# Graph attention with experts: scores of two heads by one weight load, and list tests as signs on ScalarE

## The chip, the core and the metric

The kernel runs on one core of a Trainium2 chip. The core has engines with queues of their own, which meet through semaphores: PE multiplies matrices into PSUM, with weight loads counted apart as PEld; DVE and POOL work on vectors; ACT applies functions element by element; SP (SyncE) mainly starts transfers (DMA). A transfer by a list of row numbers (a gather) is started by POOL. The metric is the device time of the whole program in microseconds (us). The kernel before takes 2405.32 us, the median of three runs from 2403.5 to 2418.53.

## What is computed

A layer of graph attention over 4096 nodes with 512 features, then a mixture of experts, both with a residual. Cut to what matters:

```python
# x: (4096, 512), adj: (4096, 4096) of zeros and ones
def attention(n, adj, Wks, Wqs, Wvs, Wo):            # 8 heads of 64
    adj = maximum(adj, eye)
    q, k, v = (einsum('nd,hdk->hnk', n, W) for W in (Wqs, Wks, Wvs))
    scores = einsum('hqk,hmk->hqm', q, k) * 64 ** -0.5
    scores = scores + 0.01 * eye - 1e16 * (1 - adj)
    return einsum('hqm,hmk,hko->qo', softmax(scores), v, Wo)

x = x + attention(layernorm(x), adj, ...)
x = x + experts(layernorm(x), ...)                   # top 2 of 8, GELU
```

The adjacency matrix is sparse, and its density falls from the first nodes to the last. The kernel works on 32 tiles of 128 queries and visits only the keys that a query of the tile has as neighbours.

## The kernel before

**Stage one** makes keys, values and queries, and beside that a list of keys for each tile of queries. It runs in 64 slots: four slots of each eight project keys and values of 128 tokens, four project queries and normalize the next tokens. An adjacency tile of 2 MB is loaded every 13/8 slots. DVE reduces it, two slots later, to flags: has this key a neighbour in the first 64 queries, in the last 64? Keys are then listed in three sections: those of the first half alone, those of both, those of the second half alone.

A list is made for four tiles at a time (a group). From running counts of the flags along the 32 keys that a partition holds (`x_g`) and the count before each partition (`base`), a list slot's row is found by a product: `started` has a one where partition p has begun at list slot s, and `dx` holds the step of each quantity from one partition to the next.

```python
def count_3(g):
    b = ...                                     # keys before partition p, by section
    nc.vector.scalar_tensor_tensor(lo, hi, -float(P), b, op0=ALU.mult, op1=ALU.add)   # L419
    ...
    base[g] = b

def steps(g):
    nc.tensor.matmul(pd, step, x_g, start=True, stop=False, ...)
    nc.tensor.matmul(pd[:, 1:], corner, x_g[:, :2], start=False, stop=True, ...)
    nc.tensor.matmul(pe, step, x_g[:, 2], start=True, stop=True)
    dx = lp.tile([P, 4, G, NX], BF16, tag="dx", ...)
    nc.scalar.copy(dx[:, :3], pd)
    nc.scalar.copy(dx[:, 3], pe)

def begun(i):                                   # L457
    for k, (t0, t1) in enumerate(ranges(i)):    # up to three ranges of list slots
        nc.gpsimd.tensor_scalar(
            started[i, k], slots[:, t0 * P : t1 * P], base[g][:, k, j : j + 1], None,
            op0=ALU.is_ge,
        )

def list_rows(i, k):                            # L476, on PE
    of = [(0, 0)] if h == 0 else [(2, 3)] if h == 1 else [(0, 0), (1, 1), (2, 2)]
    for n, (q, r) in enumerate(of):
        nc.tensor.matmul(pr[:, t, :], started[i, q][:, s], row_x[g][:, r, j, :], ...)

def list_keys(i, k):                            # from L486, on DVE
    ...
    nc.vector.tensor_copy(key_of[:, to], key)   # L502
    nc.vector.tensor_scalar_add(mask_of[:, u], k, float(i * (N + 1)))      # L510
    # or, for a half: nc.vector.tensor_scalar(mask_of[:, u], k, 2.0, ...)  # L512
```

A group's list takes eight slots. In each, the first part comes ahead of the slot's projections, and what the function returns comes behind them:

```python
def lists_at(g, s):
    if s == 0:
        count_1(g)
        return [lambda: count_2(g)]
    if s == 1:
        count_3(g); begun(i)
        return [lambda: steps(g)]
    if s == 2:
        begun(i + 1)
        return []
    if s == 3:
        return [lambda: rows(i)]
    if s == 4:
        keys(i); begun(i + 2)
        return [lambda: rows(i + 1)]
    ...
```

Once a list is ready, POOL gathers some of its mask rows in advance (`pack`, up to three a slot), and SP writes them to DRAM in one piece, to be loaded later without a gather. `load_adj`, L345, starts from SP at the head of a slot; `neighbours`, L352, is the reduction.

**Attention** goes through the listed keys of each tile in steps of 128, after a step for the tile's own keys. A step in a one-sided section (a half step) has 64 queries, the others have 128. `AHEAD` steps before, the keys and values (`kv`) and the mask are fetched. PE then turns the keys (`pk`, L893), multiplies them with the queries (`s`, L922), and after the exponential on ACT (L932) and the mask on DVE (L941) multiplies the result with the values (`po`, L954):

```python
def load_q(i):
    q_in[i] = qp.tile([P, NP, P], F32, tag="q", ...)      # NP = 4 pairs of heads
    nc.sync.dma_start(out=q_in[i], in_=qT_d[:, :, ts(i, P)])

def scores(n):
    s = [ps_s.tile([P, NP, P], F32, tag="s", ...) for r in range(2)]
    for p in range(NP):
        for r in range(2):                                # head 2p + r
            rows = slice(r * KD, (r + 1) * KD)            # its 64 rows
            nc.tensor.matmul(                             # L922
                part(s[r], i, c)[:, p, :], k[rows, p, :], q_in[i][rows, p, q],
                start=True, stop=True,
            )
    ...
    for r in range(2):
        nc.scalar.activation(e[:, r * NP : (r + 1) * NP], part(s[r], i, c), AF.Exp)  # L932

def values(n):
    for p in range(NP):
        for r in range(2):
            h = 2 * p + r
            nc.tensor.matmul(                             # L954
                po[i][r * KD : (r + 1) * KD, p, q], v[:, ts(h, KD)], e[:, r * NP + p, :], ...
            )
    nc.vector.tensor_add(acc[i][:, :, q], acc[i][:, :, q], e)
```

Each product of 32-bit numbers stands in the profile as two loads of weights and two multiplications. At a tile's end, `sums` (L979), `rb` (L992: four products of 128 rows by 128 columns with 128 columns streamed) and `py` (L1001) finish it. Routing of the tokens and the **experts** follow (from L1295), which the change leaves alone.

Of the kernel before, what the change touches and what calls it, by code (L numbers as in the profile page):

```python
# [10 lines left out]
F32 = mybir.dt.float32  # L11
# [9 lines left out]
P = 128  # L21
# [22 lines left out]
def kernel(  # L44
# [174 lines left out]
    def load_q(i):  # L219
        q_in[i] = qp.tile([P, NP, P], F32, tag="q", name=f"q_{i}")  # L220
        nc.sync.dma_start(out=q_in[i], in_=qT_d[:, :, ts(i, P)])
# [46 lines left out]
    with tc.tile_pool(name="wqkv", bufs=1) as wp, tc.tile_pool(name="p1", bufs=3) as work, tc.tile_pool(  # L268
# [39 lines left out]
        )  # L308

# [21 lines left out]
        def list_constants():  # L331
            nc.vector.tensor_sub(step, ident, step)
            nc.vector.tensor_mul(other, other, part)
            nc.vector.tensor_scalar(other, other, -1.0, 1.0, op0=ALU.mult, op1=ALU.add)
            nc.vector.memset(again_c, 1.0)
            nc.vector.memset(again_c[:, :, :, 0:1], 0.0)
            nc.vector.tensor_scalar_mul(corner, corner, -1.0)
            for k in range(KV // D):
                nc.sync.dma_start(out=kv_d[N : N + 1, ts(k, D)], in_=blank[:1, :D])
# [60 lines left out]
        def count_3(g):  # L400
# [24 lines left out]
            base[g] = b  # L425

        def steps(g):

# [3 lines left out]
            nc.tensor.matmul(  # L432
                pd[:, 1:], corner, x_g[:, :2], start=False, stop=True, skip_group_check=True
            )
            pe = ps_l.tile([P, G, NX], F32, tag="l", name=f"pe_{g}")
            nc.tensor.matmul(pe, step, x_g[:, 2], start=True, stop=True)
            dx = lp.tile([P, 4, G, NX], BF16, tag="dx", name=f"dx_{g}")
            nc.scalar.copy(dx[:, :3], pd)
            nc.scalar.copy(dx[:, 3], pe)
# [7 lines left out]
        def begun(i):  # L447

            g, j = divmod(i, G)
            for k, (t0, t1) in enumerate(ranges(i)):  # L450
                if t0 == t1:
# [5 lines left out]
                nc.gpsimd.tensor_scalar(  # L457
                    started[i, k], slots[:, t0 * P : t1 * P], base[g][:, k, j : j + 1], None,
                    op0=ALU.is_ge,
# [5 lines left out]
        def list_rows(i, k):  # L465
# [4 lines left out]
            for t in range(m):  # L470
                h = half_of(i, t0 + t)

                of = [(0, 0)] if h == 0 else [(2, 3)] if h == 1 else [(0, 0), (1, 1), (2, 2)]
# [8 lines left out]
        def list_keys(i, k):  # L482
# [21 lines left out]
            for h, u0, u1 in ((0, 0, a), (None, a, b), (1, b, listed[i])):  # L504
                u0, u1 = max(u0, t0), min(u1, t0 + m)
                if u0 < u1:
                    u = slice(at[i] + u0, at[i] + u1)
                    k = key[:, u0 - t0 : u1 - t0]
                    if h is None:
                        nc.vector.tensor_scalar_add(mask_of[:, u], k, float(i * (N + 1)))  # L510
                    else:
                        nc.vector.tensor_scalar(  # L512
# [27 lines left out]
        def lists_at(g, s):  # L540

            def rows(i):
                for k in range(len(chunks(i))):
                    list_rows(i, k)
                    if k:
                        list_keys(i, k - 1)
# [3 lines left out]
            if s == 0:  # L550
                count_1(g)
                return [lambda: count_2(g)]
            if s == 1:
                count_3(g)
                begun(i)
                return [lambda: steps(g)]
            if s == 2:
                begun(i + 1)
                return []
            if s == 3:  # L560
                return [lambda: rows(i)]
            if s == 4:
                keys(i)
                begun(i + 2)
                return [lambda: rows(i + 1)]
            if s == 5:
                keys(i + 1)
                begun(i + 3)
                return [lambda: rows(i + 2)]
            if s == 6:  # L570
                keys(i + 2)
                return [lambda: rows(i + 3)]
            keys(i + 3)
            return []
# [40 lines left out]
        def pack():  # L615
            i, c = ready.pop(0)
            m = work.tile([P, P], F32, tag="mask", bufs=6, name=f"pm_{i}_{c}")
# [5 lines left out]
        lists_from = {13 * (g * G + G - 1) // 8 + 3: g for g in range(NTB)}  # L623
        for u in range(8 * NTB + 1):
# [4 lines left out]
            for k in range(8):  # L629
                if u - k in lists_from:  # L630
                    due += lists_at(lists_from[u - k], k)
# [19 lines left out]
            if u - 2 in load_at:  # L651
                neighbours(load_at[u - 2])
                if load_at[u - 2] == NT - 1:
# [4 lines left out]
                    q_cm = tc.tile_pool(name="q", bufs=2, side="right")  # L658
                    qp = q_cm.__enter__()
                    load_q(0)  # L660
# [6 lines left out]
            if u - 8 in lists_from:  # L667
                g = lists_from[u - 8]
                ready += [
                    (i, c) for i in range(g * G, g * G + G) for c in range(listed[i])  # L670
                    if c % 5 in (1, 3)
                ]
# [29 lines left out]
    def route_1(m, l, pool, name):  # L702
# [4 lines left out]
        ahead = pool.tile([P, m, E, E], F32, tag="ahead", name=f"ahead_{name}")  # L707
        nc.vector.tensor_tensor(ahead, other, own, op=ALU.is_gt)
        same = pool.tile([P, m, E, E], F32, tag="same", name=f"same_{name}")
# [133 lines left out]
    with tc.tile_pool(name="p2a", bufs=2) as two, tc.tile_pool(  # L843
# [38 lines left out]
        def load_x(i):  # L882
            x_in[i] = two.tile([P, D], F32, tag="xt", name=f"xr_{i}")
# [21 lines left out]
        def part(t, i, c):  # L905

            if half_of(i, c) is None:
                return t
            heads = t.shape[1]
            t = t.rearrange("p h q -> p (h q)")[:, : heads * QH]  # L910
            return t.rearrange("p (h q) -> p h q", h=heads)

        def scores(n):

            i, c = items[n]
            s = [ps_s.tile([P, NP, P], F32, tag="s", name=f"s{r}_{i}_{c}") for r in range(2)]
            k = kT.pop(n)
            q = queries(i, c)
            for p in range(NP):
                for r in range(2):  # L920
                    rows = slice(r * KD, (r + 1) * KD)
                    nc.tensor.matmul(  # L922
                        part(s[r], i, c)[:, p, :], k[rows, p, :], q_in[i][rows, p, q],
# [495 lines left out]
```

## Time and profile before

The profiled execution spans 2203.7 us.

| Engine | busy us | share of the span | instructions |
|---|---|---|---|
| PE | 2040.5 | 93% | 20620 |
| PEld | 1366.7 | 62% | 20620 |
| DVE | 1319.2 | 60% | 2387 |
| ACT | 870.1 | 39% | 1842 |
| POOL | 1242.8 | 56% | 1072 |

DMA moves 481.71 MB, 219 GB/s on the mean. These shares are means over stages of different kinds, so the profile is best read by stretches of time. A line of instructions in it names the kernel's line, engine, operation, output and inputs, shapes and count; then the busy time in us and the mean of one in ns, and the idle time of the engine ahead of it with what ended that. A line of the timeline begins with start and length in us. PE's clock is given as the share of full speed that was granted. The end of a multiplication is modelled, so distances from start to start are more to be trusted than lengths.

### The profile page before, as it was taken

The page shows a single profiled execution, that of the slowest core. Times are in us where ns is not written, and L with a number is a line of the kernel's source. Part 1 is how long each engine was busy: PE and PEld are TensorE (multiplying, and loading weights), DVE is VectorE, ACT ScalarE, POOL GpSimd, SP SyncE. Part 2 cuts the span into 40 slices and gives each one's busy share as a digit, 9 for nine tenths or more (in the row PEclk, how much of TensorE's full clock was granted, in tenths as well). Part 3 has the DMA queues.
Part 4 walks back from the last instruction along what each step waited for, and adds up shares of the span by engine and source line. Part 5 has one row for each costly group of instructions (what it writes and reads, how often), then busy time and mean ns, then how long its engine had stood idle before and what let it go on. Part 6 is the DMA issues. An engine that isn't in the chain of part 4 may idle for free. (4 is left out here: it accounts for less than half of the span.)

```text
span 2203.7 us, 52479 instructions
## 1 busy us (share of the span) xinstructions
PE 2040.5 (93%) x20620; PEld 1366.7 (62%) x20620; DVE 1319.2 (60%) x2387; ACT 870.1 (39%) x1842; POOL 1242.8 (56%) x1072
## 2 busy tenths in 40 slices
PE   7877879899999999999999999999829999999998
PEld 3333334348888888888788878777614444444444
DVE  4888586724887767777677777777723222333232
ACT  2121211124666646655556555656412222222222
POOL 1769888885888657678676766667412112111112
PEclk9988988896999989999999999999959999999999
DMA  7737787847788868878788878878475556555554
GB/s 281 301 127 234 258 294 261 263 120 236 247 260 273 273 216 275 281 239 282 247 268 266 267 249 248 264 234 252 165 257 127 134 131 136 136 134 140 137 136 96
DMA packets 215039, 481.71 MB, mean 219 GB/s; under 512 B 49618, under 2 KB 81874, under 8 KB 210692
## 3 DMA queue, kind: packets, MB, share of 16 engines
q0 software_dynamic: 79232, 242.18, 37.1%
q1 hardware_dynamic: 134404, 234.01, 33.7%
q8 instruction: 168, 2.75, 0.5%
q10 hardware_dynamic: 1152, 2.10, 0.3%
q14 instruction: 83, 0.68, 0.1%
HBM read 400.59 MB, written 77.58 MB: 217 GB/s over the span
## 5 line engine op out<-in xcount | busy, mean ns | idle before, releaser
L225 POOL DMA_INDIRECT kv<-kv_d,key_of x363 | 430.4, 1186 | 231.8 <-PE po L954 136.4
L941 DVE TENSOR_TENSOR e<-e,mask 128x512 f32<-128x512 f32 (+1 forms) x363 | 322.6, 889 | 204.0 <-ACT e L932 200.4
L922 PE MATMUL s<-q,kT 64*128 64x64 f32 (+1 forms) x5808 | 409.4, 282 | 2.7 <-ACT acc L932 2.7
L1354 POOL DMA_INDIRECT out_dram<-y,r x71 | 110.6, 1558 | 474.0 <-ACT h L1324 124.7
L922 PEld LDWEIGHTS s<-q,kT 64*128 64x128 f32 x5808 | 373.4, 196 | 2.9 <-ACT acc L932 2.9
L896 ACT COPY kT<-pk 128x512 f32<-128x512 f32 x395 | 232.1, 588 | 285.1 <-PE pk L893 277.3
L932 ACT ACTIVATE e<-s 128x256 f32<-128x256 f32 (+1 forms) x726 | 297.1, 461 | 101.5 <-PE s L922 98.6
L960 DVE TENSOR_TENSOR acc<-acc,e 128x512 f32<-128x512 f32 (+1 forms) x363 | 320.4, 883 | 1.4 <-PE po L954 1.4
L954 PE MATMUL po<-e,kv 128*64 128x64 f32 (+1 forms) x5808 | 311.3, 251 | 0.0
L225 POOL DMA_INDIRECT mask<-in_adjT_dram,mask_of x230 | 257.7, 1121 | 71.9 <-issue 50.0
L457 POOL TENSOR_SCALAR started<-slots,base 128x384 bf16<-128x384 int16 (+12 forms) x96 | 229.0, 2401 | 76.6 <-DVE longer L407 75.7
L954 PEld LDWEIGHTS po<-e,kv 128*64 128x64 f32 x5808 | 246.4, 141 | 34.7 <-issue 0.8
L1318 PE MATMUL ph<-w,xT 128*128 x568 | 258.3, 598 | 0.7 <-ACT xT L207 0.7
L1347 PE MATMUL py<-w,hT 128*128 x568 | 255.6, 593 | 0.9 <-DVE hT L1332 0.9
L352 DVE TENSOR_REDUCE flags<-adjT 128x64 f32<-128x4096 f32 x32 | 141.2, 4413 | 81.2 <-DMA adjT<-in_adjT_dram 81.2
L1352 DVE TENSOR_TENSOR y<-py,bb 128x512 f32<-128x512 f32 x71 | 49.1, 692 | 225.6 <-PE py L1347 184.2
L893 PE MATMUL pk<-ident,kv 64*128 64x64 f32 x2904 | 172.4, 240 | 11.4 <-ACT kT L896 11.0
L893 PEld LDWEIGHTS pk<-ident,kv 64*128 64x128 f32 x2904 | 122.0, 142 | 77.0 <-issue 47.2
L1318 PEld LDWEIGHTS ph<-w,xT 128*128 128x128 f32 x568 | 103.2, 192 | 104.1 <-issue 103.0
L1347 PEld LDWEIGHTS py<-w,hT 128*128 128x128 f32 x568 | 102.5, 190 | 104.0 <-issue 102.8
L225 POOL DMA_INDIRECT pm<-in_adjT_dram,mask_of x133 | 130.5, 981 | 41.5 <-issue 33.6
L1353 ACT ACTIVATE y<-y,gate 128x512 f32<-128x512 f32 x71 | 51.2, 722 | 213.1 <-DVE y L1352 213.1
(589 smaller groups left out, 2405.3 us busy)
## 6 DMA issues: line engine op xcount, KB each, us to landing
adjT<-in_adjT_dram SPq DMA_DIRECT2D x32, 2048.0 KB
bb<-in_L_ffn_b_dram SPq DMA_DIRECT2D x142, 256.0 KB
r<-xs_d SPq DMA_DIRECT2D x71, 258.0 KB
kv_d<-kv SPq DMA_DIRECT2D x32, 512.0 KB
xt<-in_x_dram SPq DMA_DIRECT2D x32, 256.0 KB
qT_d<-qT SPq DMA_DIRECT2D x8, 1024.0 KB
q<-qT_d SPq DMA_DIRECT2D x32, 256.0 KB
xr<-in_x_dram SPq DMA_DIRECT2D x32, 256.0 KB
```

The lines of the kernel that those rows point to most:

```text
L225: nc.gpsimd.indirect_dma_start(out=to, out_offset=None, in_=src, in_offset=bass.IndirectOffsetOnAxis(ap=of[:, at[i] + c : at[i] + c + 1], ...
L352: nc.vector.tensor_reduce(flags[g][:, :, j, :], adj_in.pop(i).rearrange("p c (h q) -> p h c q", h=2), axis=AX.X, op=ALU.max,)
L457: nc.gpsimd.tensor_scalar(started[i, k], slots[:, t0 * P : t1 * P], base[g][:, k, j : j + 1], None, op0=ALU.is_ge,)
L893: nc.tensor.transpose(pk[:, r, ts(p, KD)], kv[n][half, ts(p, P)], ident[half, half])
L896: nc.scalar.copy(kT[n].rearrange("k p (r j) -> k r p j", r=2), pk[:, :, : NP * KD].rearrange("k r (p j) -> k r p j", p=NP),)
L922: nc.tensor.matmul(part(s[r], i, c)[:, p, :], k[rows, p, :], q_in[i][rows, p, q], start=True, stop=True,)
L932: nc.scalar.activation(e[:, r * NP : (r + 1) * NP], part(s[r], i, c), AF.Exp)
L941: nc.vector.tensor_mul(e, e, m.unsqueeze(1).to_broadcast(e.shape))
L954: nc.tensor.matmul(po[i][r * KD : (r + 1) * KD, p, q], v[:, ts(h, KD)], e[:, r * NP + p, :], start=(c < 0 and p == 0), stop=(c == listed[i ...
L960: nc.vector.tensor_add(acc[i][:, :, q], acc[i][:, :, q], e)
L1318: nc.tensor.matmul(ph, xTs[b][:, c, :], w1[:, bass.ds(es[b], 1), c, :], start=(c == 0), stop=(c == DC - 1),)
L1347: nc.tensor.matmul(py, hTs[b][:, c, :], w2[:, bass.ds(es[b], 1), c, :], start=(c == 0), stop=(c == HC - 1),)
```

## The change

It has two parts, with some moves of buffers around them.

In attention, the queries are laid in SBUF with zeros beside them: for each pair of heads there are two blocks of 128 queries, one with the first head's 64 rows filled and the other 64 zero, one the other way round. A half step then needs one weight load for the keys of two heads (128 rows) and streams both heads' 64 queries behind it. [...] one exponential covers it. Full steps keep a product for each head. The heads lie in their natural order in `e`.

In stage one, the tests `started` become signs on ACT (-1 or 1), and the steps are halved to fit: a sum of ones times steps equals half the sum of signs times steps plus half the whole, which `top` and `around` add. `mask_of` is worked out on POOL. A list takes nine slots, and PE gets what DVE or ACT made in an earlier slot. The reduction of an adjacency tile comes three slots behind its load instead of two.

The diff, cut to its core:

```diff
     def load_q(i):
-        q_in[i] = qp.tile([P, NP, P], F32, tag="q", name=f"q_{i}")
-        nc.sync.dma_start(out=q_in[i], in_=qT_d[:, :, ts(i, P)])
+        q_in[i] = q_two[i % 2]
+        for r in range(2):
+            rows = slice(r * KD, (r + 1) * KD)
+            nc.sync.dma_start(out=q_in[i][rows, :, r, :], in_=qT_d[rows, :, ts(i, P)])
 ...
-            base[g] = b
+            past_b = lp.tile([P, 3, G], F32, tag="past_b", name=f"past_b_{g}")
+            nc.vector.tensor_scalar(past_b, b, -1.0, 0.5, op0=ALU.mult, op1=ALU.add)
+            base[g] = past_b
 ...
             nc.tensor.matmul(
+                pd[:, 0], top, x_g[:, 2], start=False, stop=False, skip_group_check=True
+            )
+            nc.tensor.matmul(
                 pd[:, 1:], corner, x_g[:, :2], start=False, stop=True, skip_group_check=True
             )
-            nc.tensor.matmul(pe, step, x_g[:, 2], start=True, stop=True)
+            nc.tensor.matmul(pe, around, x_g[:, 0::2], start=True, stop=True)
-            nc.scalar.copy(dx[:, :3], pd)
-            nc.scalar.copy(dx[:, 3], pe)
+            nc.scalar.mul(dx[:, :3], pd, 0.5)
+            nc.scalar.mul(dx[:, 3:], pe, 0.5)
 ...
-                nc.gpsimd.tensor_scalar(
-                    started[i, k], slots[:, t0 * P : t1 * P], base[g][:, k, j : j + 1], None,
-                    op0=ALU.is_ge,
+                nc.scalar.activation(
+                    started[i, k], slots[:, t0 * P : t1 * P], AF.Sign,
+                    bias=base[g][:, k, j : j + 1],
                 )
 ...
-                        nc.vector.tensor_scalar_add(mask_of[:, u], k, float(i * (N + 1)))
+                        nc.gpsimd.tensor_scalar_add(mask_of[:, u], k, float(i * (N + 1)))
 ...
-        def lists_at(g, s):
+        def lists_of(g):
 ...
+            yield lambda: count_1(g), None
+            yield None, lambda: count_2(g)
+            yield counted, None                 # count_3(g), begun(i)
+            yield lambda: begun(i + 1), lambda: steps(g)
+            yield None, lambda: rows(i)
+            for j in range(G):
+                def then():
+                    keys(i + j)
+                    if j + 2 < G:
+                        begun(i + j + 2)
+                yield then, (lambda: rows(i + j + 1)) if j + 1 < G else None
 ...
-        lists_from = {13 * (g * G + G - 1) // 8 + 3: g for g in range(NTB)}
+        lists_from = {13 * (g * G + G - 1) // 8 + 4: g for g in range(NTB)}
 ...
-            if u - 2 in load_at:
-                neighbours(load_at[u - 2])
+            if u - 3 in load_at:
+                neighbours(load_at[u - 3])
 ...
+                    q_two = [qp.tile([P, NP, 2, P], F32, name=f"q_{k}") for k in range(2)]
+                    for t in q_two:
+                        for r in range(2):
+                            rows = slice(r * KD, (r + 1) * KD)
+                            nc.gpsimd.memset(t[rows, :, 1 - r, :], 0.0)
 ...
         def scores(n):
 ...
+            if full:                            # 64 rows for each head, as before
 ...
+                        nc.tensor.matmul(
+                            s[r][:, p, :], k[rows, p, :], q_in[i][rows, p, r, :],
+                            start=True, stop=True,
+                        )
 ...
+            else:
+                s = ps_s.tile([P, NP, 2, QH], F32, tag="s", name=f"s_{i}_{c}")
+                for p in range(NP):
+                    nc.tensor.matmul(
+                        s[:, p], k[:, p, :], q_in[i][:, p, :, q], start=True, stop=True
+                    )
+                nc.scalar.activation(e, s.rearrange("p a r q -> p (a r) q"), AF.Exp)
 ...
-            if c == 2:
+            if c == min(7, listed[i] - 1):
                 load_x(i)
```

Space for the wider queries comes from single buffers: `ahead` and `same` in the routing, the attention output `o`, the residual rows `xr` (loaded later in the tile, the last tile with its own buffer), and five instead of six buffers for the packed masks.

## The prediction

> **What bounds the kernel now.** I read the busy times by stage first. The profiled execution (2203.7 us) has three stages: projections and lists of keys up to 497 us, where attention's first transpose of keys starts; attention up to 1593 us; routing and experts after that. The change touches the first two. Columns: stretch, its length, busy us (instructions) of PE, weight loads, DVE, ACT and POOL, granted clock, DMA share, GB/s.
>
> ```profile
> core 0: us, PE busy (x) PEld busy (x) DVE busy (x) ACT busy (x) POOL busy (x), PEclk, DMA share, GB/s
> 20.00:497.00 477.00, 404.17 (x1584) 190.81 (x1583) 321.61 (x604) 95.93 (x169) 364.06 (x234) 0.91 0.68 234
> 551.00:1593.00 1042.00, 1019.96 (x16639) 850.05 (x16636) 777.46 (x1226) 608.72 (x1392) 720.72 (x615) 0.98 0.80 252
> ```
>
> The two stages differ. In stage one PE is busy for 404 of 477 us, at a clock of 0.91, POOL for 364 and DVE for 322: they take turns waiting. In attention PE is busy 98% of the time at 0.98, and nothing else is near full.
>
> Next come the waits of stage one (engine and line, whom it waited for, us in total, times, longest).
>
> ```profile
> DVE flags L352 <- DMA adjT<-in_adjT_dram: 81.2, 20, 10.6
> ...
> DVE within L486 <- PE pr L476: 43.3, 8, 11.8
> PEld L476 <- POOL started L457: 40.7, 23, 4.6
> ```
>
> PE's list products wait for POOL's tests `started`, and DVE's reduction waits for the 2 MB adjacency load. In the timeline each load is issued only 8 to 10 us before its reduction starts, though its buffer has been free for some 20 us: the SP queue is in order and stands behind the previous slot's packs, which POOL delivers. Then the groups by shape, and the timeline at the first list:
>
> ```profile
> L457 POOL TENSOR_SCALAR started<-slots,base 128x896 bf16<-128x896 int16 x17 | 42.8, 2519 | 0.1
> ```
>
> ```profile
> 70.00 0.55 DVE L417 TENSOR_REDUCE hi<-most 128x12 f32<-128x384 f32 x1
> 70.58 7.42 DVE L419 SCALAR_TENSOR_TENSOR lo<-hi,base 128x12 f32<-128x12 f32 x1
> 77.93 0.34 DVE L420 CAST x<-hi 128x12 bf16<-128x12 f32 x1
> ```
>
> A 12-column operation that normally takes 0.16 to 0.6 us lasts 7.42 us. It ends when POOL's first test ends: that test began at 69.55 and took 8.66 us. So the tests cost twice, on POOL and on DVE.
>
> Last, PE's timeline in attention: two half steps, and a full-array product (`rb`: 128 rows of contraction, 128 columns, eight instructions) that has the form of the new scores.
>
> ```profile
> 1203.39 0.46 PE L893 MATMUL pk<-ident,kv 64*128 64x64 f32 x8
> 1203.69 1.06 PE L922 MATMUL s<-q,kT 64*128 64x64 f32 x16
> 1204.68 0.69 PE L954 MATMUL po<-e,kv 128*64 128x64 f32 x16
> 1205.30 0.46 PE L893 MATMUL pk<-ident,kv 64*128 64x64 f32 x8
> ...
> 1211.70 0.69 PE L954 MATMUL po<-e,kv 128*64 128x64 f32 x16
> 1212.32 1.16 PE L992 MATMUL rb<-rinv,spread 128*128 128x128 f32 x8
> ```
>
> Start to start, a half step takes 0.30 + 0.99 + 0.62 = 1.91 us. No engine's wait lies between these groups; this stage is a chain of PE groups.
>
> [...] pairs of half-row loads of 128 columns step by 0.112 us although only 64 columns stream, the same step as full steps (128 streamed) and as `rb`. [...] from `pk` to `s`, both of 64 rows by 128, last start to first start is 0.059 us; from `po` (64 columns streamed, other mode) to `pk` or to `rb` it is 0.152. [...] `Exp` over 256 elements takes 383 ns and over 512 takes 595, so 0.83 ns an element.
>
> **Part 1, the tests move from POOL to ACT as signs.** POOL loses 96 instructions, 229 us in all. ACT gains them: the three ranges of all tiles add up to 80,768 elements; at 0.83 ns that is 67 us, and 96 fixed costs of about 0.28 us (170 ns from the two `Exp` sizes, and about 0.11 for the bias, taken from `xn`, which has two such operands and takes 821 ns against 588 for a copy) are 27 us. So 94 us on ACT, which is busy for only 96 of 477. DVE gets back [...]: summing over its groups how much each instruction exceeds its shortest twin gives about 75 us. It also hands the key-to-row sums `mask_of` to POOL (lines 510 and 512, 40 us with waits). DVE thus falls from about 330 to about 215 us in this stage.
>
> **Part 2, lists in nine slots, PE a slot behind DVE, the reduction one slot later.** PE finds its tests and counts ready. Gaps over 1 us in PE's timeline between 20 and 497 us add up to 77 us. The clock of 0.91 means some 88 us at half rate, brought on by these gaps, costing about 35 us of PE time beyond the gaps. Without both, stage one would end at 497 - 77 - 35 = 385 us. The adjacency load gets one more slot (about 7 us), more than nearly all waits of the 81.2 us. Three things keep it from 385. First DMA: up to 437 us it is busy for 0.73 x 437 = 319 us at full rate, and 380 GB/s is the most that a stretch of 12.5 us shows. PE's own floor for that part is 385 - 60 = 325. [...] about 365, and with the last 60 us, which have few gaps now, about 425. Second, in slots of the query projection ACT has a sign group (2.3 to 3.1 us), `xn` 0.82 and two copies 1.2, about 5 us, against 4.5 us for PE: up to 1 us in some 16 slots, partly inside the first. Third, two list slots come later, where PE is busy anyway. I take an end between 415 and 445 and choose 427: **70 us less**.
>
> **Part 3, half steps' scores over 128 rows.** 229 of the 363 listed steps are half ones (count them from the code's lists). Sixteen instructions of 64 rows become eight of 128 rows with 128 columns streamed, half of them zeros. By `rb` the step stays 0.112 us, so the seven steps keep about 0.78 us: nothing is gained, because the old pairs already ran side by side. Two costs are new. `pk` to `s` now changes the mode: 0.152 instead of 0.059, +0.093. And after a change the first load of 128 columns lies open: the second `rb` matmul starts 0.213 after the first, then every 0.112: +0.101. From `s` to `po` the mode changed before too (0.202). That is +0.19 us x 229 = **44 us more** on the full engine.
>
> On ACT, two `Exp` of 383 ns become one of 595: 229 x 0.171 = 39 us less, but ACT is busy 609 of 1042 us and ends little. [...] PE's excess over its usual group times in attention is 43 us, part of it waits for ACT's key copies; I give 5 us of it back. Busier rows might also shorten the slow stretches (41 us at half clock between 510 and 551, another 44 later): 5 us. So attention: +34 us.
>
> **Part 4, the rest.** Each tile's query load becomes two transfers of half the partitions; there is one tile in some 34 us (1096 / 32): hidden. Four memsets on POOL: under 5 us, once. The later `xr` load still has over ten steps. Single buffers of `o`, `ahead` and `same`: their readers finish within five steps of a tile of nine or more. The experts stay.
>
> **Sum.** -70 + 34 = -36. The timed 2405.3 us lies 200 us above the profiled span; I take that as constant. 2405 - 36 = **2369 us**.
>
> **Rivals.** A: the switch of mode costs nothing, [...] or rows that work fully keep the clock up. [...] Against: every one of 31 `po`-to-`rb` pairs shows it. Attention stays equal or gains 10, and the time is about 2325. B: stage one is held by DMA or by ACT in the new order. For it: 0.9 of DMA in many stretches after 250 us; ACT must end signs before it frees PSUM for the projections. Then stage one ends near 455 and the time is about 2397. C: POOL's `mask_of`, waiting for DVE's keys, stalls the gathers behind it in its queue, so the packs, the SP queue and with them the adjacency loads come late again. For it: one queue in order. Against: POOL gets 229 us back. It would make the time about 2385.
>
> **Range and chances.** Stage one may bring 40 to 95, attention cost -10 to 50. The ends are unlikely together: 2325 to 2412 for 8 in 10. Faster by 2% needs 2357, 12 us below my value, within the spread of some 30 us: 0.35. Slower by 2% needs stage one to bring nothing: 0.03. Within 2%: 0.62.
>
> **What would show it.** Right: DVE's wait for `adjT` and PE's for `started` gone; no short DVE instruction over 2 us; attention's first `pk` at 415 to 445 us; half scores at about 1.1 us start to start with 0.15 ahead; attention 20 to 45 us longer at equal clock. Wrong: half scores in under 0.95 us with 0.06 ahead (A), DMA or ACT as the new name ahead of PE in stage one (B), `mask_of` waits on POOL followed by late loads (C).

## The result and the profile after

The changed kernel takes **2309.5 us** (median of 4 runs, 2305.8 to 2316.0) beside 2408.3 us for the kernel before (2403.5 to 2418.5): ratio 0.959, 95% interval 0.955 to 0.963. The prediction was 2369 us with a range down to 2325, so the gain of 99 us is more than twice the 36 us that were worked out.

The stages first: stretch, its length, busy us (instructions) of PE, weight loads, DVE, ACT, POOL, granted clock, DMA share, GB/s. This is the view by stretches of the changed kernel.

```profile
20.00:449.00 429.00, 386.11 (x1591) 183.47 (x1589) 266.64 (x512) 181.30 (x265) 155.65 (x235) 0.95 0.76 262
561.00:1686.00 1125.00, 1044.54 (x14015) 837.33 (x14011) 729.70 (x1152) 553.07 (x1107) 671.77 (x584) 0.98 0.75 221
```

Stage one now ends at 449 us, not 497: POOL is down from 364 to 156 us busy, ACT up from 96 to 181, the clock up from 0.91 to 0.95. But attention, from 449 to 1686 us, takes 1237 us where the profile shown ahead of the prediction has 1087. Read against that profile, the change looks like a loss of 100 us, and the timing says the opposite.

The reason is that those two profiles do not belong together. **The runs fall into two kinds of session** (a session: the runs made together on one chip, with the kernel before among them): in some the kernel before takes 2199 to 2207 us, in others 2408 to 2423, steadily within each. The profile of before came from a session of the first kind, its timed runs and the profile of the changed kernel from the second. The expectations below call such a session a machine; that is too much, because chips with the same number showed both kinds. I call them quick and slow sessions here. Totals and attention are compared within one kind only. Stage one is also compared across them, because the kernel before ends it at 497 us in a quick session and at 499 in a slow one.

The waits of stage one in the changed kernel, from 20 to 440 us (engine and line, whom it waited for, total us, times, longest):

```profile
POOL mask_of L530 <- DVE key L517: 128.3, 12, 90.2
POOL pm L228 <- DMA packed_h<-pm: 80.0, 18, 10.0
DVE within L504 <- PE pr L494: 62.3, 13, 20.5
...
ACT started L475 <- DVE past_b L434: 54.4, 8, 16.5
DVE flags L359 <- DMA adjT<-in_adjT_dram: 52.3, 12, 10.0
...
PEld pt_a L206 <- ACT xn L200: 36.5, 12, 11.1
```

PE's wait for `started` is gone, as meant. The reduction's wait for `adjT` is not: 52.3 us of 81.2 stay, and 69.4 in b4, the same kernel in a quick session. One wait is new: ACT's signs wait for DVE's `past_b`. PE's wait for the `xn` that stands behind those signs in ACT's queue has grown from 14.2 us to 36.5. POOL's `mask_of` waits for DVE's keys, which is the sign that rival C named; but 121 of the 128 us, 90 of them in one wait, come before 180 us, at the first lists.

PE's timeline of a half step in attention (start, us, operation):

```profile
905.44 0.46 PE L917 MATMUL pk<-ident,kv 64*128 64x64 f32 x8
905.83 1.16 PE L964 MATMUL s<-q,kT 128*128 128x128 f32 x8
906.92 1.09 PE L987 MATMUL po<-e,kv 128*64 128x128 f32 x16
```

From `pk` to `s` it is 0.39 us (0.30 before), from `s` to the next group 1.09 (0.99 before): the 0.19 us of Part 3, to the hundredth. The medians over 227 of the half steps show where it stands: from the last `pk` to the first `s` 0.153 us (0.059 before), from the first `s` to the second 0.213, and 0.112 between the others.

### The profile page after: what moved, and what is told of

The parts are those of the page before. It is cut to its first block, busy times and chain, and to the rows that moved or that the text cites. A ratio compares the mean times of both kernels' runs of the same rounds, so it can differ in the third digit from the quotient of the medians.

```text
span 2307.7 us, 48617 instructions
## 1 busy us (share of the span) xinstructions
PE 2102.1 (91%) x18796; PEld 1389.0 (60%) x18796; DVE 1266.7 (55%) x2297; ACT 933.3 (40%) x1709; POOL 1030.9 (45%) x1080
## 5 line engine op out<-in xcount | busy, mean ns | idle before, releaser
L228 POOL DMA_INDIRECT kv<-kv_d,key_of x363 | 405.8, 1118 | 384.4 <-PE po L987 220.5
L987 PE MATMUL po<-e,kv 128*64 128x64 f32 (+1 forms) x5808 | 322.4, 250 | 18.2 <-issue 17.9
L228 POOL DMA_INDIRECT mask<-in_adjT_dram,mask_of x234 | 282.3, 1206 | 72.9 <-issue 63.4
L987 PEld LDWEIGHTS po<-e,kv 128*64 128x64 f32 x5808 | 251.9, 139 | 70.1 <-issue 25.8
L964 PE MATMUL s<-q,kT 128*128 128x128 f32 x1832 | 276.2, 295 | 3.1 <-issue 2.7
L964 PEld LDWEIGHTS s<-q,kT 128*128 128x128 f32 x1832 | 230.8, 197 | 19.4 <-issue 3.5
L917 PE MATMUL pk<-ident,kv 64*128 64x64 f32 x2904 | 177.5, 239 | 49.0 <-ACT kT L920 30.1
L957 ACT ACTIVATE e<-s 128x512 f32<-128x512 f32 x268 | 146.9, 597 | 72.1 <-PE s L952 30.1
L967 ACT ACTIVATE e<-s 128x512 f32<-128x512 f32 x229 | 137.9, 602 | 79.4 <-PE s L964 43.9
L359 DVE TENSOR_REDUCE flags<-adjT 128x64 f32<-128x4096 f32 x32 | 141.0, 4408 | 52.3 <-DMA adjT<-in_adjT_dram 52.3
L952 PE MATMUL s<-q,kT 64*128 64x128 f32 x2144 | 160.2, 283 | 4.6 <-issue 2.6
```

The lines of the kernel that those rows point to most:

```text
L228: nc.gpsimd.indirect_dma_start(out=to, out_offset=None, in_=src, in_offset=bass.IndirectOffsetOnAxis(ap=of[:, at[i] + c : at[i] + c + 1], ...
L359: nc.vector.tensor_reduce(flags[g][:, :, j, :], adj_in.pop(i).rearrange("p c (h q) -> p h c q", h=2), axis=AX.X, op=ALU.max,)
L917: nc.tensor.transpose(pk[:, r, ts(p, KD)], kv[n][half, ts(p, P)], ident[half, half])
L952: nc.tensor.matmul(s[r][:, p, :], k[rows, p, :], q_in[i][rows, p, r, :], start=True, stop=True,)
L957: nc.scalar.activation(e.rearrange("p (a r) q -> p r a q", r=2)[:, r], s[r], AF.Exp)
L964: nc.tensor.matmul(s[:, p], k[:, p, :], q_in[i][:, p, :, q], start=True, stop=True)
```

## Experiments

"Stage one" is the time up to attention's first `pk`, "attention" the time from there to its last `pk`.

### The two parts alone, in a quick session

The kernel before once more; the part in stage one alone (scores as before); the scores alone; the changed kernel again. The scores alone were also run with six mask buffers:

```
-            m = work.tile([P, P], F32, tag="mask", bufs=5, ...)      # b3, as in the change
+            m = work.tile([P, P], F32, tag="mask", bufs=6, ...)      # b5, as before the change
```

> The kernel before once more, for a second profile. Its profiled run spanned 2204 us, its timed runs 2405, while the changed kernel has 2308 in both. Theory F (feed): in the usual runs PE waits inside attention for instructions or for something else that no semaphore shows, and the first profile caught a run without it: the span is now near 2400, stage one still ends near 497, and attention takes about 1290 us instead of 1096 with many idle stretches of PE put down to issue. Theory S (all stages): the usual run is slower everywhere by the same 9%: stage one ends near 540, attention takes about 1190, the experts 660. Theory U: the first profile was right for attention, and the span is 2204 again.

> Stage one of the changed kernel with attention's scores as before (sixteen 64-row instructions for every step). Theory F: scores with fewer instructions gained in attention, so the lists alone bring only what their stage shows (497 - 449 = 48 us): about 2360. The predicted working (scores cost PE 0.19 us in each of 229 half steps, 44 us, and lists bring the rest): about 2265.

> Attention of the changed kernel (zeros beside the queries, one load for two heads in half steps, one exponential) with stage one as before. Theory F: about 2355, some 50 us faster than before, although each half step's score group takes 0.19 us longer from start to start. The predicted working: about 2445, 40 us slower.

> The changed kernel once more, on whatever machine the kernel before is measured beside it. The earlier pair was 2408 and 2310; the three kernels before this one were measured where the kernel before takes 2199. Theory F (PE is short of instructions on some machines, and the change gained by having fewer of them): where the kernel before takes about 2199, the changed one takes about 2183, which is 2199 less 43 of the lists plus 27 that attention took longer with the new scores; where it takes about 2408, the changed one takes about 2310 again, with PE idle inside groups for issue. Theory G (the gain is the change's own everywhere): a ratio of 0.96 again, so about 2110 beside 2199.

> The scores alone, with six instead of five buffers for the packed masks. With five, stage one ended at 533 us instead of 497, and POOL waited for the packed masks' stores. If the lost buffer is the cause, stage one ends near 497 again and the ratio to the kernel before falls from 1.027 to about 1.012, which is attention's own loss of 27 us. If the two half-partition query loads or the memsets are the cause, it stays at 1.027.

| run | us | ratio to before, 95% | stage one | attention |
|---|---|---|---|---|
| b1, before | 2198.8 | 1.000 (0.999 to 1.002) | 497 | 1076 |
| b2, lists alone | 2156.5 | 0.981 (0.976 to 0.985) | 443 | 1089 |
| b3, scores alone, 5 mask buffers | 2259.5 | 1.027 (1.022 to 1.032) | 533 | 1103 |
| b5, scores alone, 6 mask buffers | 2224.9 | 1.012 (1.010 to 1.014) | 500 | 1103 |
| b4, changed | 2176.5 | 0.989 (0.987 to 0.991) | 450 | 1107 |

In a quick session the change brings 22 us, not 99: 47 us are won in stage one and some 25 given back in attention by the scores. The stage times come from one profile each. Over all quick profiles attention takes 1076 to 1090 us with the old scores and 1103 to 1107 with the new ones, so its loss lies between 13 and 31 us. The sixth mask buffer is worth 33 us in stage one to a kernel whose POOL still does the tests (b3 against b5). b2 and b4 have five; what a sixth would bring with the tests on ACT was not run.

### Stage one: which step brings it, and what holds it

c1 takes the nine slots without moving the tests. c2 takes b2 and lets the stores of the packed masks follow one slot later, with eight buffers. c3 takes b2 and asks for a list's first two sign groups one slot later. c4 does both. In short:

```
c1  before, with lists_of, lists_from + 4, neighbours(load_at[u - 3])
c2 -nc.sync.dma_start(out=packed_at(i, c), in_=mask_part(m, i, c))
   +stores.append((m, i, c))        # issued in the next slot; bufs=8
c3 -counted: count_3(g), begun(i)      then: begun(i + 1), steps(g)
   +counted: count_3(g)                then: begun(i), begun(i + 1), steps(g)
```

> The nine slots alone: lists in nine slots, PE a slot behind DVE, the reduction three slots behind its load; the tests stay on POOL as ones and zeros, mask_of on DVE, scores as before. If POOL's tests (229 us of its 477) [...] are what holds stage one, the slots alone bring at most 15 us: stage one ends at 480 to 490 us. If the order of the slots alone removes the waits, it ends near 445, as with the whole list part.

> The list part with scores as before, and the stores of packed masks started by SP a slot after their gathers, from eight buffers instead of five. Theory Q (queue): the 2 MB adjacency loads are issued only some 9 us ahead of their reduction because SP, in order, waits for the gathers behind the packed masks; with late stores they are issued 15 us ahead or more, DVE's 69 us of waits for them fall under 20, and stage one ends near 415 instead of 443 us. Theory D (transfer rate): DMA is as good as full in stage one, and it ends near 440 again.

> The list part with scores as before, and the first tile's signs one slot later, so that ACT too takes only what DVE made a slot earlier. PE's remaining gaps in stage one (47 us) all stand behind ACT's normalized tokens, and ACT stands in the signs' wait for DVE's past_b (55 us). If that is a cause of its own, the gaps fall by half and stage one ends near 425 us. If DVE is late because of its loads, ACT waits elsewhere and it ends near 440.

> Late stores and later signs together, on the list part with scores as before. Theory Q with the signs' wait: stage one near 400 us, the whole about 40 us below the lists alone, a ratio of 0.962 to the kernel before where that takes 2199 us. Theory D: no better than 0.98.

| run | us | ratio to before, 95% | stage one | DVE waits for adjT |
|---|---|---|---|---|
| c1, slots alone | 2210.5 | 1.002 (1.000 to 1.003) | 501 | 50 |
| c2, late stores | 2141.2 | 0.970 (0.966 to 0.973) | 422 | 23 |
| c3, later signs | 2170.7 | 0.982 (0.978 to 0.987) | 451 | 88 |
| c4, both | 2125.8 | 0.963 (0.958 to 0.968) | 411 | 26 |

**The slots alone bring nothing.** The waits of c1 show why: PE's wait for POOL's tests has only grown, from 39.8 us before to this (both up to 440 us).

```profile
PEld L476 <- POOL started L457: 62.1, 35, 6.0
```

The held-up DVE instructions stayed too. Below, a 12-column operation of DVE: shortest, median and longest of 8, in ns, first in c1 (tests on POOL), then in the changed kernel (tests on ACT).

```profile
L419 DVE SCALAR_TENSOR_TENSOR lo<-hi,base x8: 170/173/7418, 81.0 to 451.5; 128x12 f32<-128x12 f32 x8
```

```profile
L426 DVE SCALAR_TENSOR_TENSOR lo<-hi,base x8: 170/170/172, 80.4 to 406.1; 128x12 f32<-128x12 f32 x8
```

With the tests off POOL the longest falls from 7418 to 172 ns: DVE is held up while the tests run on POOL, and not without them. Summed over DVE's groups in stage one, what its instructions take beyond their shortest twin is 75 us before, 82 in c1 and 4 in b2 and in the changed kernel. What b2 has beyond c1 is this move, and `mask_of` on POOL instead of DVE (it has one mask buffer less, too); the two together bring the gain of 58 us in stage one. Whether they bring as much in the old slots was not run.

**The load comes late because of what stands ahead of it in the queue, not because of its slot.** Over the last 20 of the 32 adjacency loads, the median from the issue to the start of the reduction (the lead) is 9.0 us in b1 and 9.3 in b2, although the reduction moved a slot. A masks' store waits in the SP queue for its gathers, and the next loads stand behind it. In c2 the lead is 16.5 us, and the wait for `adjT` falls from 61 to 23. But c2 changes two things, the turn of the stores and the number of buffers, and a run below (d2) has the late stores with five buffers and no gain. SP's wait for the gathers at these stores, up to 420 us, in b2, in c2 and in d2:

```profile
SPq L627 <- DMA pm<-in_adjT_dram,mask_of: 179.7, 65, 7.8
```

```profile
SPq L634 <- DMA pm<-in_adjT_dram,mask_of: 54.8, 23, 7.3
```

```profile
SPq L639 <- DMA pm<-in_adjT_dram,mask_of: 147.7, 47, 8.3
```

With five buffers POOL's gathers wait in turn for a store to free one: 122 us in b2 and 140 in d2, beside 60 in c2. So late stores and eight buffers together bring the loads forward. Late stores with five buffers do not, and eight buffers alone were not run.

The signs' turn alone gains nothing (c3): the wait for the load grows to 88 us instead. Together with c2's moves it ends stage one at 411. The waits that are left in c4:

```profile
DVE flags L356 <- DMA adjT<-in_adjT_dram: 26.3, 7, 10.6
...
PEld pt_a L206 <- ACT xn L200: 24.0, 13, 5.4
...
ACT started L472 <- DVE past_b L431: 6.6, 3, 3.7
```

### Slow sessions: which part gains, and on what

First a row of 2048 tiny products behind the kernel before, to see whether PE's instructions come at a limited rate; and the changed kernel with both moves of c4, but five mask buffers, since more do not fit beside the wider queries.

```
+for k in range(2048):
+    nc.tensor.matmul(fed, below, ones[:, :32], start=(k == 0), stop=(k == 2047))
```

> The kernel before with 2048 small bf16 products (a load of 128 columns and 32 streamed columns each) in one row at its end, to see how fast PE can be given instructions when nothing else runs. In stage one such pairs step by 25 ns in groups of 16 to 60. If PE is fed without limit, 2048 pairs take 51 us without a gap. Theory F needs a limit near what attention asks: then the row runs at 25 ns for the first hundred or so and falls to stretches between stalls of 0.6 to 0.7 us, as in the changed kernel's first profile, with a sustained rate of some 30 to 50 instructions per us (attention before asks 42 in half steps, 80 in 1.91 us, and with the new scores 30).

> The changed kernel with late stores (five buffers) and later signs. Where the kernel before takes about 2200 us: 2177 less 33 = 2144, or a few us more for the lost buffers. Where it takes about 2408: 2310 less 33 = 2277.

Both fell into a slow session (before: 2412.7 us). The tiny products start every 25 ns. After one pause of 3.6 us near the start there is a pause of 0.28 to 0.58 us each 128 products. That is some 70 instructions per us sustained (4096 in 60.1 us), faster than the 42 per us of a half step before (80 in 1.91 us). So PE running by itself meets no steady limit near what attention asks. Attention of this kernel before took 1302 us with the same instructions that take 1076 in a quick session. d2 took 2335.5 us (0.966, 0.962 to 0.971), against some 2277 expected and slower than the changed kernel's 0.959. Its stage one takes 458 us, so with five buffers the two moves did not shorten it: the expectation failed.

Then the parts alone again, in a slow session (before: 2423.2 us): the same kernels as b5, b2 and c4.

> The scores alone with six mask buffers, once more. If the machine is one where the kernel before takes about 2400 us: by the theory that PE is kept short of instructions there, fewer matrix instructions pay, attention is 50 to 70 us shorter than before's and the ratio is 0.97 to 0.98; by the rival that the gain there comes from the lists, it is 1.01 as on the other machine. Where before takes about 2200 us both expect 1.01.

> The stage-one part alone with the scores of before, once more. Where before takes about 2400 us: by the theory of PE's instructions only stage one gains, 45 to 50 us, ratio 0.98; by the rival (the gain comes from the lists) 0.96. Where before takes about 2200 us both expect 0.98.

> The lists with late stores and later signs and the scores of before, once more. Where before takes about 2400 us: stage one 85 us shorter, attention as before's, ratio 0.965, so level with the changed kernel's 0.96. Where before takes about 2200 us: 0.963 as measured.

e1 took 2383.6 us (0.983, 0.979 to 0.987), e2 2376.4 (0.979, 0.973 to 0.985), e3 2353.4 (0.968, 0.961 to 0.975). Stage one takes 504 us in e1, 449 in e2 and 429 in e3, which has c4's eight buffers. So here the scores **gain** 40 us, where they lost 26. The attention stages, with two sums over them: the time for which only half the clock was granted, and "stalls", the steps of over 0.5 us from one PE product's start to the next. In each sum of stalls about 33 us are ordinary steps of `py`, which take 0.52 us.

| attention of | session | us | half clock, us | stalls, us |
|---|---|---|---|---|
| before (b1) | quick | 1076 | 55 | 65 |
| scores alone (b5) | quick | 1103 | 27 | 59 |
| changed (b4) | quick | 1107 | 31 | 63 |
| before (d1) | slow | 1302 | 283 | 155 |
| lists alone (e2) | slow | 1307 | 287 | 161 |
| scores alone (e1) | slow | 1251 | 79 | 163 |
| changed (the result) | slow | 1237 | 79 | 155 |

In slow sessions PE stands still more, with no engine or transfer named as releaser. PE's timeline in e2:

```profile
654.88 1.06 PE L938 MATMUL s<-q,kT 64*128 64x64 f32 x16
...
658.02 0.73 PE L970 MATMUL po<-e,kv 128*64 128x64 f32 x7
659.16 0.36 PE L970 MATMUL po<-e,kv 128*64 128x64 f32 x5 [0.40 <-issue]
659.88 0.50 PE L970 MATMUL po<-e,kv 128*64 128x64 f32 x4 [0.36 <-issue]
...
661.37 0.49 PE L909 MATMUL pk<-ident,kv 64*128 64x64 f32 x4 [0.25 <-issue]
661.55 2.31 PE L938 MATMUL s<-q,kT 64*128 64x64 f32 x16
663.80 1.12 PE L970 MATMUL po<-e,kv 128*64 128x64 f32 x16
```

Three stops within a few microseconds, in the middle of groups, marked "issue"; then the same scores that took 1.06 us take 2.31, and `po` 1.12 instead of 0.69: the clock has halved, and stays so for 10 us. The theory had been that fewer instructions meet fewer stops. **The table speaks against it**: with 7% fewer products recorded in the stage, e1 stalls as long as e2 (163 and 161 us), and the changed kernel as long as d1 (155). What differs is the clock that follows, 79 instead of 285 us at half rate. e2 has 31 stretches at half rate, of 9.3 us on the mean, and e1 has 17, of 4.6 us. The stalls in the 7 us ahead of one have a median of 2.7 us in e1 and 1.8 in e2. So with the new scores the clock falls less often and comes back sooner. In quick sessions it only comes back sooner: b1 has 5 stretches and b5 has 6. The granted clock shows it (last but two of the columns), attention in e2 and then in e1:

```profile
560.00:1756.00 1196.00, 1113.91 (x15817) 913.06 (x15818) 737.57 (x1163) 576.49 (x1330) 671.02 (x590) 0.91 0.69 210
```

```profile
561.00:1755.00 1194.00, 1102.65 (x14711) 884.10 (x14707) 767.29 (x1195) 580.79 (x1159) 694.90 (x610) 0.97 0.73 218
```

### What holds the clock: instructions, rows or streamed columns

The new scores differ from the old in three ways: fewer instructions, 128 rows instead of 64, 128 streamed columns instead of 64. f1 runs three forms in rows by themselves, each burst followed by the same pause: "half" (pairs of 64 rows, 64 columns, as before), "wide" (the same pairs with 128 columns) and "full" (128 rows, 128 columns, as in the change). g1 and g2 put "wide" into the kernel before and into c4: the half steps' scores are computed over all 128 queries of the tile, and only the 64 wanted are read.

```
f1 +for count, times in ((8, 30), (16, 18), (32, 10), (48, 8)):
   +    for form in ("half", "wide", "full"):      # 96 full steps ahead of each
   +        for _ in range(times):
   +            nc.scalar.mul(mr[:, :, :1], outs[0][:, :, :1], 0.01)   # the pause
   +            steps_of(form, count)
g1 -part(s[r], i, c)[:, p, :], k[rows, p, :], q_in[i][rows, p, q],
   +s[r][:, p, :], k[rows, p, :], q_in[i][rows, p, :],
   -nc.scalar.activation(e[...], part(s[r], i, c), AF.Exp)
   +nc.scalar.activation(e[...], s[r][:, :, q], AF.Exp)
```

> Rows of products after the last output, each group of 8, 16, 32 or 48 steps followed by a pause of some 0.7 us (PE waits for ACT to rewrite an operand): half = a pair of 64-row products over 64 columns (the half steps before), wide = the same pair over 128 columns, full = one product of 128 rows over 128 columns (the half steps after). All step by about 0.11 us at full clock. If the clock follows how many columns PE streams, half falls to half rate at a length at which wide and full keep the full clock. If it follows the rows or the number of instructions, wide goes with half. If it follows only the pauses, all three fall at the same length.

> The kernel before with half steps' scores over all 128 queries (16 instructions as before; the further 64 columns are computed and not read). Instructions as many as before, streamed columns as in the changed kernel. If streamed columns keep the clock up: time at half rate in attention falls (on the slower machine from 285 to under 120 us and attention 70 to 90 us shorter, ratio 0.965; where before takes 2200, from some 70 to 30 us, 15 to 20 us shorter, ratio 0.992), with no added mode switch. If what helps is fewer instructions or full rows: the time at half rate stays, ratio 1.00.

> Lists with late stores and later signs, and the half steps' scores over all 128 queries. By the theory of streamed columns the gains add: ratio 0.955 where before takes 2200 us, 0.935 where it takes 2400 us. By the rival it equals the lists alone: 0.963 and 0.968.

> The same kernel as g2_both_wide. On a machine where the kernel before takes about 2400 us, the theory of streamed columns expects under 120 us at half rate in attention (287 with the lists alone) and a ratio of 0.93 to 0.94; the rival (fewer instructions help there) expects 0.968, as the lists with both moves. Where before takes 2200 us both expect 0.959, as measured.

The timeline of f1's shortest bursts, half, wide and full:

```profile
2264.46 3.68 PE L1395 MATMUL row<-mr,wr 64*128 64x64 f32 x32 [0.34 <-ACT mr L1403]
2268.48 3.68 PE L1395 MATMUL row<-mr,wr 64*128 64x64 f32 x32 [0.34 <-ACT mr L1403]
...
2390.01 2.06 PE L1395 MATMUL row<-mr,wr 64*128 64x128 f32 x32 [0.34 <-ACT mr L1403]
2392.40 2.06 PE L1395 MATMUL row<-mr,wr 64*128 64x128 f32 x32 [0.34 <-ACT mr L1403]
...
2480.86 2.05 PE L1390 MATMUL row<-mr,wr 128*128 128x128 f32 x16 [0.33 <-ACT mr L1403]
2483.24 2.05 PE L1390 MATMUL row<-mr,wr 128*128 128x128 f32 x16 [0.33 <-ACT mr L1403]
```

And its clock over the three rows (the same columns as the stages above):

```profile
2226.00:2336.00 110.00, 100.49 (x928) 95.39 (x928) 0.00 (x0) 5.00 (x29) 0.00 (x0) 0.54 0.00 1
2364.00:2432.00 68.00, 58.58 (x919) 53.22 (x916) 0.00 (x0) 4.96 (x28) 0.00 (x0) 1.00 0.01 2
2457.00:2525.00 68.00, 58.78 (x460) 53.45 (x460) 0.00 (x0) 4.98 (x29) 0.00 (x0) 1.00 0.00 1
```

This settles it for rows by themselves. With bursts of 1.8 us and pauses of 0.6, half falls to half rate and stays there (0.54), while wide, with as many instructions and the same rows, keeps the full clock (1.00), as full does (1.00). **There it is the streamed columns:** at full clock half streams 64 of them in each step of 0.11 us, and wide 128 in the same step. With bursts of 3.6 us half keeps the clock too (1.00 from 2550 to 2619 us). In attention the half-rate stretches last 3.4 us or multiples of it, up to 41.0 us in the profile of before and 13.7 in that of the changed kernel. What sets these lengths was not shown.

In the kernel, g1 has 34 us at half rate in attention instead of b1's 55. One profile each would be little to go by, but the eight quick profiles with the old scores have 55 to 89 us, and the six with the new scores or with "wide" have 27 to 34. g1 took 2198.5 us (0.998, 0.996 to 0.999), where 0.992 was expected. The scores have the form of the `pk` ahead of them (64*128) and start 0.30 us after it, as before, but they are 0.05 us longer than before's 0.99:

```profile
1216.21 0.46 PE L893 MATMUL pk<-ident,kv 64*128 64x64 f32 x8
1216.51 1.11 PE L922 MATMUL s<-q,kT 64*128 64x128 f32 x16
1217.55 0.69 PE L954 MATMUL po<-e,kv 128*64 128x64 f32 x16
```

From `pk` to `s` 0.30, from `s` to `po` 1.04: over 229 steps 12 us, about what the clock gives back (half of 21 us). g2 takes 2113.3 us (0.959, 0.955 to 0.963) and h1, the same kernel once more, 2116.6 (0.961, 0.957 to 0.964), beside 0.963 for c4 and 0.989 for the changed kernel: the shortest time of all in quick sessions. Attention takes 1079 us with 31 us at half rate, c4's 1083 with 72. Both came to quick sessions, so what it takes in a slow one was not measured, and that streamed columns alone hold the clock there is not shown.

## Why the prediction was wrong

**Part 1 held in its mechanism.** ACT went from 96 to 181 us (worked out: 190), POOL from 364 to 156 (208 less, 229 counted). The 96 signs add up to 95 us (94 worked out): from 384 to 3200 elements they take 0.603 to 2.962 us, so 0.84 ns an element and 0.28 us besides, where 0.83 from `Exp` and 0.28 had been put in as estimates. DVE's short instructions are no longer held up: what they take beyond their shortest twins, 75 us, fell to 4. b2 against c1 shows that the stage-one gain hangs on this part, `mask_of` included. DVE's relief was sized too large: it is busy for 267 us instead of 322, so 55 less where 115 were worked out.

**Part 2 was sized at 70 us and measured 48.** Its two terms were gaps of 77 us and 35 us of clock, all to vanish, with DMA as the new floor at 425 us. Of the gaps 48 us are left and of 89 us at half rate 44: 29 + 22 = 51, near the 48 measured. The clock did go with the gaps: each of the 14 half-rate stretches in the profile of before begins within 10 us behind a gap of 2.1 us or more in PE's timeline, and each of the 7 in the changed kernel behind one of 1.9 or more. The term that failed is "the adjacency load gets one more slot, more than nearly all waits". Over the last 20 loads the lead grew from 8.8 to 11.4 us (10.2 in b4), not by 7, because the load stands behind stores that wait for POOL's gathers, and these wait for buffers. That is rival C's kind of fault, with the stores and their buffers in place of `mask_of`: in c2 `mask_of` waits longer, 155 us, and the loads come early. The reading behind the term was too simple as well: a lead of 8 to 10 us is that of the later loads, and loads 5 to 10 had 18 to 39 us before. The prediction has no term for the mask buffer that the change takes away. Nor did DMA set the floor: c4 ends at 411, and the step from streams of 319 and 325 us to 365, on which the 425 rest, was my estimate.

**Part 3's working held, in its two costs.** Measured are 0.39 and 1.09 us for the worked-out 0.39 and 1.09, which makes 44 us for 229 steps. But the term for the clock, "busier rows might also shorten the slow stretches ...: 5 us", was the small one in the text and is the large one in the result. (The stretch of 41 us that it names lies from 500 to 541 us.) In quick sessions it is worth 14 us (28 us less at half rate, b5 against b1), and with the 44 leaves 30: measured 27. In slow sessions there are 204 us less at half rate, so about 102 us, and 44 - 102 = -58: measured -51 (e1 against d1), and -65 in the changed kernel. By f1 it is the columns that do it, not the rows.

**The step that decided the miss** is the last line of the sum: "The timed 2405.3 us lies 200 us above the profiled span; I take that as constant." It was not a constant outside the stages. The 200 us lie in attention (1302 against 1087 us), where stalls (about 92 us more) and the half clock that follows them (198 us more, so 99 us) account for some 190 of the 215. A part of the kernel that the change touches was that much longer than in the profile that I worked from. In a quick session the sum as it stood, -70 + 34 = -36, comes near the -22 measured, partly because both parts were sized too large; the slow session gives -99.

**Open** stays why PE stands marked "issue" for longer in the attention of some sessions. A row of products by itself steps on there, some 70 instructions per us (d1), and fewer instructions did not bring fewer stalls (e1). A DMA queue that the profile calls "instruction" (q8) moves 16 KB at a time, in attention 137 times beside 34,984 products and weight loads in the profile of before and 122 times beside 31,069 in that of the changed kernel: one transfer for 255 of them in both. These take 1.00 us in the first, a quick session, and 0.98 in the second, a slow one (medians), so the transfers themselves are not slower there. Whether PE waits for them is not shown.

## What to carry to other kernels

When the timed median and the profiled span differ by much more than the spread of the runs, find the stage that holds the difference before working out any change; a profile of another session prices a stage wrongly. Where short products take the same step for 64 streamed columns as for 128 (0.11 us here), streaming more of them may keep the full clock through short pauses (1.00 instead of 0.54 in f1); in the kernel it cost 0.05 us in a group of 1 us. When a load comes late, look at what stands ahead of it in its queue, and at what that waits for in turn: here a later turn for the stores brought nothing until there were buffers for it.

## What was not expected of the hardware

Pairs of 64-row products over 64 columns, in bursts of 1.8 us with pauses of 0.6, ran at half rate for 93% of 110 us, and never at all over 128 columns. The same program's attention took 1076 or 1302 us by session, with stalls of mostly 0.6 to 0.7 us marked "issue", while stage one took 497 and 499 us, and what follows attention 619 to 632 us in quick profiles and 622 to 626 in slow ones (d1 and f1, with rows added at the end, aside).
